# The down product of a layer on TensorE: eight of its ten tiles by seven products at two levels, over halves of the whole sequence, with streamed weights

## The chip, the cores and the metric

The kernel runs on one core of a Trainium2 chip. The core has TensorE (matmuls, out of SBUF into PSUM), VectorE, ScalarE and GpSimd for everything else, and SyncE (SP), whose queue issues most transfers between HBM and SBUF. The metric is the device time of one execution in microseconds (us).

## The reference

The input x has 8 sequences of 1024 rows of 512 numbers, all float32. With xn the normalised x, the layer computes

```python
xn = _layernorm(x, axis=-1)
s = _L0_attn_ref(xn, ...)           # gated linear attention with decay, 3 heads, then @ Wo * out_scale
gate, up = ghost(xn, gate_idx), ghost(xn, up_idx)   # w = lut[idx]; x @ w.T ; 512 -> 1376
h = silu(gate) * up
g = _silu(ghost(h, down_idx))       # 1376 -> 512: the down product
x = x + s * g
```

The weights of the three "ghost" products are looked up in a table of 16 numbers by integer indices. The down product multiplies h, 1024 x 1376 in each sequence, by a matrix of 1376 x 512.

## The kernel before, in words

The program has two phases. **Phase 1** runs the attention for the eight sequences (`project`, `chunks`): TensorE is kept in a written-out order, and between its steps `build_some` advances a generator, `ffn_weights`, which looks up the weights of the feed-forward part on VectorE (`look_up`: three bit masks, a shift, eight leaves, seven predicated copies), forms sums of their blocks on GpSimd, and stores them in HBM. `build_some` takes one step at each place; what is left of the generator after the last sequence runs at once. The results of the attention go to HBM too (`bl_d`), as do the normalised x and sums of its blocks (`xs_d`).

**Phase 2** runs the feed-forward part for one sequence after the other. The 1376 rows of h are ten tiles of 128 and a tail of 96. `quads` makes tiles 0 to 7 (in all but the first sequence 8 and 9 too), `single` the tail, each with fewer products than the plain way: a product of two matrices in 2 x 2 blocks takes seven block products instead of eight, in Winograd's form, where sums of blocks take the place of some operands. In `quads` this is done at two levels. One outer product of the seven is a `Node`: it has four PSUM banks, `t[0]` to `t[3]`, and its seven inner products go into them in the order 1, 5, 6, 2, 7, 3, 4. Instead of adding everything later, it starts a bank from another one: ScalarE copies t[0] to t[1] after product 1 (`first`), product 6 accumulates on that (`sixth`), ScalarE copies t[1] to t[2], and VectorE adds the copy `e` of product 5 to t[1] and t[3] (`sixth`, `seventh`). The first two products of the following node are placed inside the node.

Then comes the down product, `down_pair`, for the chunks c and c + 4 of 128 rows. The two chunks, two halves of five tiles of h, and two halves of 256 columns of the output are the 2 x 2 blocks. So there are four pairs, seven products each, five matmuls of 128 x 128 by 128 x 256 each (L976). The weights with their sums, `wd_sb`, stay in SBUF through phase 2. The sums of blocks of h are made by `sums` on VectorE (L956 to L959), for the first pair from inside `single`: `at_last` is called there, between the products 7 and 3 of the tail of h, and ahead of the two VectorE operations (L710, L713) that read the last products. The ScalarE Silu L711 reads what L710 writes, GpSimd's L714 multiplies. After the down products come a matmul with `wdt` (the tail), a Silu, a matmul `ps` of the attention's output by Wo (L998), a multiplication with it (L999), GpSimd's addition of x (L1001) and the store (L1002).

At the end `keep_order` ties every instruction of TensorE, VectorE, ScalarE and GpSimd to the one traced before it on the same engine. So these four run in the order of the program text; the order of the loads in SP's queue is left to the compiler's scheduler, except in the first part of phase 1.

PSUM has eight banks, two for each of the roles s11, s12, s21, sE. `ring` holds three buffers for streamed weights; `xs` (the x of the sequence with its sums) has one buffer, filled again once its readers are through.

Of the kernel before, what the change touches and what calls it, by code (L numbers as in the profile page):

```python
# [9 lines left out]
F32 = mybir.dt.float32  # L10
# [7 lines left out]
P = 128  # L18
# [19 lines left out]
def recurrent_block(ctx: ExitStack, tc, x, wq, wk, wv, wo, wg, decay_logits, out_scale, lut, gidx, uidx, didx, out):  # L38
# [18 lines left out]

    nc = tc.nc
# [25 lines left out]
    wd_d = [dram.tile([P, 7 * V // 2], F32, name=f"wdd{j}", tag=f"wdd{j}") for j in range(NK)]  # L84
# [28 lines left out]
    def defer(parts, issue):  # L113
        later.append([parts, issue])
# [111 lines left out]
    def ffn_weights(build, pool, pair_pool):  # L226
# [5 lines left out]

        upper = []

        def gate_up(o):
# [19 lines left out]
            defer(3, lambda: nc.sync.dma_start(out=wgu_d[o], in_=wide))  # L255
# [31 lines left out]
        def down(j):  # L287
            idx = build.tile([P, NB], I32, name="idx", tag="idx", bufs=2)
            for a in range(2):
                nc.sync.dma_start(out=idx[:, ts(a, V)], in_=didx[ts(j + a * NK, P), :])  # L290
            yield
            t = pool.tile([P, 2 * NB], F32, name="wgu", tag="wgu", bufs=2)
            yield from look_up(build, t[:, : 2 * V], idx, P, 2 * V)
            b11, b12, b21, b22, t1, t2, t4 = (t[:, ts(k, V // 2)] for k in range(7))
            nc.gpsimd.tensor_tensor(t1, b12, b11, ALU.subtract)
            nc.gpsimd.tensor_tensor(t2, b22, t1, ALU.subtract)
            yield
            nc.gpsimd.tensor_tensor(b12, b22, b12, ALU.subtract)
            nc.gpsimd.tensor_tensor(t4, b21, t2, ALU.subtract)
            defer(3, lambda: nc.sync.dma_start(out=wd_d[j], in_=t[:, : 7 * V // 2]))  # L300

        jobs = [gate_up(o) for o in range(NO)] + [down_tail()] + [down(j) for j in range(NK)]
# [333 lines left out]
    def phase_2():  # L636
        with (
# [6 lines left out]
            tc.tile_pool(name="wdp", bufs=1) as wdp,  # L644
        ):
            wd_sb = [wdp.tile([P, 7 * V // 2], F32, name=f"wd{j}", tag=f"wd{j}") for j in range(NK)]
# [5 lines left out]
            def load_x(b):  # L652

                xs = fx.tile([P, 7, 7, H], F32, name=f"xs{b}", tag="xs")
                nc.sync.dma_start(
                    out=xs[:, :, 0:4, :], in_=xs_d[b].rearrange("p (k r) (s t) -> p k (r s) t", r=2, s=2)
                )
                return xs

            def sums_of_x(xs, apart=False):  # L660

                b11, b12, b21, b22, t1, t2, t4 = (xs[:, :, k, :] for k in range(7))
                todo = [(t1, b12, b11), (t2, b22, t1), (t4, b21, t2)]
                if apart:
                    for k in (1, 6, 5, 7, 2, 3, 4):
                        n = X_OF[k]
                        todo.append((b12[:, n], b22[:, n], b12[:, n]))
                else:
                    todo.insert(2, (b12, b22, b12))
                for o, x1, x2 in todo:  # L670
                    nc.gpsimd.tensor_tensor(o, x1, x2, ALU.subtract)  # L671
                    yield
# [275 lines left out]
            def blocks(h, c):  # L948

                return [h[:, ts(k, NK), ts(cc, P)] for cc in (c, c + NC // 2) for k in range(2)]  # L950

            def sums(b, h, c):
                t = [ring.tile([P, 14, P], F32, name=f"s{b}_{c}_{k}", tag="wr")[:, : 2 * NK] for k in range(2)]
                s1, s2, s3, s4 = (t[k // 2][:, ts(k % 2, NK)] for k in range(4))
                a11, a12, a21, a22 = blocks(h, c)
                nc.vector.tensor_tensor(s1, a21, a22, ALU.add)  # L956
                nc.vector.tensor_tensor(s2, s1, a11, ALU.subtract)
                nc.vector.tensor_tensor(s3, a11, a21, ALU.subtract)
                nc.vector.tensor_tensor(s4, a12, s2, ALU.subtract)  # L959
                return s1, s2, s3, s4  # L960

            def down_pair(b, c, h, h_tail, bl, t, following):

                cc = c + NC // 2
                a11, a12, a21, a22 = blocks(h, c)
                lhs = {1: a11, 2: a12, 3: t[3], 4: a22, 5: t[0], 6: t[1], 7: t[2]}
                gx = tmp.tile([P, 4, V], F32, name=f"gx{b}_{c}", tag=("p1", "u2")[c % 2])
                g1, g2 = gx[:, 0], gx[:, 1]
                pw = tmp2.tile([P, 4, V], F32, name=f"pw{b}_{c}", tag=("u3", "e5")[c % 2])
                pe, u3 = pw[:, 0], pw[:, 1]  # L970
                for n, k in enumerate((c, cc)):
                    nc.sync.dma_start(out=gx[:, 2 + n], in_=x[b, ts(k, P), :])

                def product(ps, k, start, stop):
                    for n in range(NK):
                        nc.tensor.matmul(  # L976
                            ps,
                            lhsT=lhs[k][:, n, :],
                            rhs=wd_sb[n][:, ts(D_OF[k], H)],
                            start=start and n == 0,  # L980
                            stop=stop and n == NK - 1,
                            skip_group_check=True,
                        )

                def tail(ps, k, start):
                    m = OCH[-1][1]
                    nc.tensor.matmul(  # L987
                        ps,
                        lhsT=h_tail[:m, ts(k, P)],
                        rhs=wd_tail[:m, :],  # L990
                        start=start,
                        stop=False,
                        skip_group_check=True,
                    )

                def result(k, g, xr):
                    ps = bank("sE", f"ps{b}_{k}")
                    nc.tensor.matmul(ps, lhsT=bl[:, ts(k, P)], rhs=wo_sb, start=True, stop=True)  # L998
                    nc.vector.scalar_tensor_tensor(g, ps, osc, g, ALU.mult, ALU.mult)  # L999
                    end = (b, k) == (B - 1, NC - 1)  # L1000
                    (nc.vector if end else nc.gpsimd).tensor_tensor(g, g, xr, ALU.add)  # L1001
                    (nc.sync if end else nc.gpsimd).dma_start(out=out[b, ts(k, P), :], in_=g)  # L1002

                d1, d2, d3 = (bank(r, f"d{r}{b}_{c}") for r in ("s11", "s12", "s21"))
                product(d1[:, :H], 1, True, False)
                product(d1[:, H:], 5, False, False)
                nc.scalar.copy(pe, d1)
                product(d3[:, :H], 6, True, True)
                nc.vector.tensor_tensor(pe[:, :H], d3[:, :H], pe[:, :H], ALU.add)
                product(d1[:, :H], 2, False, False)  # L1010
                product(d3[:, H:], 7, False, True)
                nc.vector.tensor_tensor(u3[:, :H], d3[:, H:], pe[:, :H], ALU.add)
                nc.gpsimd.tensor_tensor(u3[:, H:], u3[:, :H], pe[:, H:], ALU.add)
                t = following() if following else None
                product(d1[:, H:], 3, False, False)
                tail(d1, c, False)
                nc.scalar.activation(g1[:, :H], d1[:, :H], AF.Silu)  # L1017
                nc.vector.tensor_tensor(g1[:, H:], d1[:, H:], pe[:, :H], ALU.add)
                nc.scalar.activation(g1[:, H:], g1[:, H:], AF.Silu)
                tail(d2, cc, True)  # L1020
                product(d2[:, :H], 4, False, True)
                nc.vector.tensor_tensor(g2, d2, u3, ALU.add)
                nc.scalar.activation(g2, g2, AF.Silu)
                result(c, g1, gx[:, 2])
                result(cc, g2, gx[:, 3])
                return t

            xs = load_x(0)
# [5 lines left out]
            for b in range(B):  # L1034
# [6 lines left out]
                def at_last():  # L1041
                    got.append(sums(b, h, 0))
# [8 lines left out]
                if b == 0:  # L1051
                    nc.sync.dma_start(out=wd_tail[: OCH[-1][1], :], in_=wdt_d)
                    for src, dst in zip(wd_d, wd_sb):
                        nc.sync.dma_start(out=dst, in_=src)
                quads(b, xs, h)
                single(b, NO - 1, xs, h, h_tail, at_last, tmp2)
                t = got[-1]
                more = iter(())
                for c in range(NC // 2):
                    nxt = (lambda: sums(b, h, c + 1)) if c + 1 < NC // 2 else None  # L1060
                    t = down_pair(b, c, h, h_tail, bl, t, nxt)
                    if b + 1 < B:
                        if c == 0:
                            xs = load_x(b + 1)
                            more = sums_of_x(xs)
                        else:
                            some(more, 2)
# [45 lines left out]
```

## Time and profile before

| | |
|---|---|
| time, median of 3 runs | 2159.64 us (2159.61 to 2161.4) |
| profiled execution | 2158.71 us, span 2156.9 us |
| granted TensorE clock | 1.000 |
| TensorE busy | 2147.4 us, 9486 matmul instructions |
| weight loads busy | 1647.1 us |
| VectorE, ScalarE, GpSimd busy | 1158.4, 863.9, 979.8 us |
| down products, L976 | 2240 instructions, 286.7 + 222.9 us |
| tails and results, L987 and L998 | 256 instructions, 60.2 + 60.2 us |
| matmuls of quads, L737 | 3724 instructions, 715.1 + 136.5 us |
| moved by DMA | 316.83 MB, 147 GB/s |

A row of the page reads: line, engine, operation, output <- inputs, shapes, count | busy us, mean ns of one | idle of the engine just before them, and what ended it. Matmuls are pipelined, so the mean of one (379 ns at 256 columns) is from its start to its end, while the distance from one start to the next is shorter. A float32 matmul of the program appears as two instructions. The timeline's lines give the start, the time from the first start to the last end, and the number of instructions merged. In the timeline phase 2 begins at about 605 us.

### The profile page before, as it was taken

What the parts mean: (1) busy time and instruction counts of PE and PEld (TensorE: products, weight loads), DVE (VectorE), ACT (ScalarE), POOL (GpSimd) and SP (SyncE); (2) the same over time, 40 slices, a digit from 0 to 9 for tenths busy, and PEclk for the clock granted to TensorE, in tenths of its full rate; (3) what the DMA queues carried; (4) which work ended last, traced back from release to release, by engine and by line L of the source; (5) the groups of instructions that cost most, each with busy time, mean ns of one, the idle gap of its engine ahead of it and who ended that gap; (6) DMA issues with size and microseconds to landing.
All of it is one profiled execution on the core that took longest, in us unless ns stands there. A gap on an engine that the chain in (4) does not pass through costs nothing.

```text
span 2156.9 us, 26203 instructions
## 1 busy us (share of the span) xinstructions
PE 2147.4 (100%) x9486; PEld 1647.1 (76%) x9486; DVE 1158.4 (54%) x1701; ACT 863.9 (40%) x1900; POOL 979.8 (45%) x902
## 2 busy tenths in 40 slices
PE   9999999999999999999999999999999999999998
PEld 5666666666668778778878887887788688778876
DVE  6888687678645435534543453354345435533543
ACT  3666666666334214413431441243144124413521
POOL 2554545444244553634455452455435353634442
PEclk9999999999999999999999999999999999999999
DMA  8776654545374434434442443345244334434411
GB/s 193 192 196 177 205 199 153 186 147 162 114 297 154 145 106 150 141 115 138 150 155 96 145 149 117 130 154 169 75 152 149 130 117 154 129 119 149 156 57 54
DMA packets 145943, 316.83 MB, mean 147 GB/s; under 512 B 50867, under 2 KB 76214, under 8 KB 144790
## 3 DMA queue, kind: packets, MB, share of 16 engines
q1 hardware_dynamic: 135974, 290.50, 41.7%
q0 software_dynamic: 7728, 23.86, 3.0%
q8 instruction: 75, 1.23, 0.2%
q10 hardware_dynamic: 2112, 0.79, 0.1%
q14 instruction: 54, 0.44, 0.1%
HBM read 233.98 MB, written 81.14 MB: 146 GB/s over the span
## 4 chain that ended last, share of the span: by engine, by line
PE 98%; POOL 1%; issue 0%; ACT 0%; DVE 0%; DMA 0%; POOLq 0%
PE s L737 32%; PE ds L976 22%; PE pq L410 10%; PE pv L373 8%; PE sE L737 5%; PE fs L687 4%; PE po L538 4%; PE ds L987 2%; PE ps L998 2%; PE psc L516 2%; PE pu L524 2%; PE fsE L687 2%; PE pt L366 1%; PE pk L507 1%; PE sE L780 1%; PE s L780 1%
## 5 line engine op out<-in xcount | busy, mean ns | idle before, releaser
L737 PE MATMUL s<-xs,wq 128*128 128x256 f32 x3192 | 715.1, 379 | 0.0
L737 PEld LDWEIGHTS s<-xs,wq 128*128 128x128 f32 x3192 | 605.6, 190 | 94.1 <-issue 7.0
L976 PE MATMUL ds<-wd,s 128*128 128x256 f32 x1280 | 286.7, 379 | 0.0
L976 PEld LDWEIGHTS ds<-wd,s 128*128 128x128 f32 x1280 | 243.2, 190 | 33.1
L410 PE MATMUL pq<-xnT,wqk_sb 128*128 128x512 f32 x512 | 230.3, 592 | 0.0
L976 PE MATMUL ds<-wd,h 128*128 128x256 f32 x960 | 222.9, 379 | 0.0
L976 PEld LDWEIGHTS ds<-wd,h 128*128 128x128 f32 x960 | 182.3, 190 | 52.5 <-issue 27.1
L831 POOL TENSOR_TENSOR u<-u,e 128x512 f32<-128x512 f32 x64 | 79.8, 1268 | 276.1 <-DVE u L827 276.1
L760 DVE TENSOR_TENSOR s<-s,e 128x512 f32<-128x512 f32 x133 | 93.0, 700 | 202.2 <-ACT s L759 202.2
L373 PE MATMUL pv<-wvg_sb,xnT 128*128 128x387 f32 x512 | 177.5, 488 | 0.0
L1001 POOL TENSOR_TENSOR gx<-gx 128x512 f32<-128x512 f32 x63 | 80.3, 1274 | 184.3 <-DVE gx L999 183.6
L410 PEld LDWEIGHTS pq<-xnT,wqk_sb 128*128 128x128 f32 x512 | 92.4, 190 | 92.1 <-issue 91.8
L764 DVE TENSOR_TENSOR sE<-s,e 128x512 f32<-128x512 f32 x133 | 93.0, 699 | 102.6 <-PE s L737 102.6
L737 PE MATMUL sE<-xs,wq 128*128 128x256 f32 x532 | 136.5, 379 | 0.0
L352 POOL TENSOR_SCALAR rstd<-rstd 128x1 f32<-128x1 f32 x56 | 26.8, 479 | 238.2 <-ACT junk L351 237.6
L373 PEld LDWEIGHTS pv<-wvg_sb,xnT 128*128 128x128 f32 x512 | 92.7, 190 | 54.3 <-issue 1.9
L755 ACT COPY e<-sE 128x512 f32<-128x512 f32 x133 | 77.8, 585 | 136.1 <-PE sE L737 136.1
L671 POOL TENSOR_TENSOR xs<-xs 128x1792 f32<-128x1792 f32 (+1 forms) x38 | 127.9, 3380 | 1.0
L1017 ACT ACTIVATE gx<-ds 128x256 f32<-128x256 f32 x32 | 12.3, 383 | 285.9 <-PE ds L987 285.9
L759 ACT COPY s<-s 128x512 f32<-128x512 f32 x133 | 75.8, 570 | 96.6 <-PE s L737 96.6
L748 ACT COPY s<-s 128x512 f32<-128x512 f32 x133 | 75.8, 570 | 95.8 <-PE s L737 92.1
L737 PEld LDWEIGHTS sE<-xs,wq 128*128 128x128 f32 x532 | 101.1, 190 | 13.7
(169 smaller groups left out, 3298.2 us busy)
## 6 DMA issues: line engine op xcount, KB each, us to landing
wq<-quadd SPq DMA_DIRECT2D x112, 896.0 KB, 4.4
xs<-xsd SPq DMA_DIRECT2D x8, 3584.0 KB, 11.9
wq<-quadd SPq DMA_DIRECT2D x42, 448.0 KB, 3.8
x<-in_x SPq DMA_DIRECT2D x64, 256.0 KB, 5.9
xsd<-ts SPq DMA_DIRECT2D x8, 2048.0 KB, 7.0
gx<-in_x SPq DMA_DIRECT2D x64, 256.0 KB, 2.7
out<-gx POOLq DMA_DIRECT2D x63, 256.0 KB, 2.3
ga<-gTd SPq DMA_DIRECT2D x16, 768.0 KB, 4.9
```

What stands on the lines that cost most here:

```text
L373: nc.tensor.matmul(pv, lhsT=xnT[:, v, ts(c, P)], rhs=wvg_sb[:, v, :], start=(v == 0), stop=(v == NV - 1))
L410: nc.tensor.matmul(pq, lhsT=wqk_sb[:, v, ts(j, D)], rhs=xnT[:, v, ts(hf, U)], start=(v == 0), stop=(v == NV - 1))
L538: nc.tensor.matmul(po, lhsT=lh, rhs=rh, start=(n == 0), stop=(n == len(prods) - 1))
L671: nc.gpsimd.tensor_tensor(o, x1, x2, ALU.subtract)
L687: nc.tensor.matmul(ps, lhsT=w[:, 2 * W_OF[k] + n, :m], rhs=xs[:, X_OF[k], 2 * n : 2 * n + 2, :], start=start and n == 0, stop=stop and n == 1,
L737: nc.tensor.matmul(self.t[n][:, ts(a, H)], lhsT=self.w[:, a, (0, 1, 6, 2, 3, 4, 5)[i - 1], :], rhs=self.xs[:, X_OF[self.ks[a]], D_OF[i], : ...
L755: nc.scalar.copy(self.e, self.t[3])
L760: nc.vector.tensor_tensor(self.t[1], self.t[1], self.e, ALU.add)
L764: nc.vector.tensor_tensor(self.t[3], self.t[2], self.e, ALU.add)
L831: nc.gpsimd.tensor_tensor(o[:, n], o[:, n], other[:, n], ALU.add)
L976: nc.tensor.matmul(ps, lhsT=lhs[k][:, n, :], rhs=wd_sb[n][:, ts(D_OF[k], H)], start=start and n == 0, stop=stop and n == NK - 1, skip_grou ...
L1001: (nc.vector if end else nc.gpsimd).tensor_tensor(g, g, xr, ALU.add)
```

## The change

Tiles 0 to 7 of h now take the seven products at two levels, as in `quads`. The outer blocks are halves of the sequence (512 rows), halves of the eight tiles (four each), halves of the output's columns (256). Each of the seven outer products is a `DownNode` with seven inner products over 256 rows, two tiles and 128 columns; in each inner product four matmuls of 128 x 128 by 128 x 128. The tiles 8 and 9 enter at the outer level only (`rest`), eight matmuls of the same size per node. A node's weights, 896 KB, are loaded into `ring` when it is set up. Its left operands that are sums come from VectorE: `sum_of` (outer, 128 x 2560 in three parts) and `four_of` (inner, four sums of 512 elements), issued one at a time between the steps of the node ahead; `s2` becomes the operand of node 3 on GpSimd. The sums needed first are made by `sums_ahead`, which is called where `sums` was. The results of the nodes are gathered in `cl` and `cu`; the tails and results of all eight chunks follow the nodes. The x of the following sequence is loaded in four parts and its sums are made in pieces.

In phase 1 the sums of the second level are added to the building of the down weights, and the stores of `wgu_d` for tiles 0 to 7, eight of them, are left out.

```diff
+    wd_d = dram.tile([P, 7, 2, 7 * P], F32, name="wdd", tag="wdd")
+    wdl_d = dram.tile([P, 7 * V // 2], F32, name="wdld", tag="wdld")
...
-            defer(3, lambda: nc.sync.dma_start(out=wgu_d[o], in_=wide))
+            if o >= 4 * NQ:
+                defer(3, lambda: nc.sync.dma_start(out=wgu_d[o], in_=wide))
...
-        def down(j):
+        def down(rows, e, ends):
...
+            nc.gpsimd.tensor_tensor(pair[:, :, 0], b12, b11, ALU.subtract)
+            yield
+            nc.gpsimd.tensor_tensor(b12, b22, b12, ALU.subtract)
+            defer(3, lambda: nc.sync.dma_start(out=to[:, :, 0:2, :], in_=up))
+            yield
+            nc.gpsimd.tensor_tensor(pair[:, :, 1], b22, pair[:, :, 0], ALU.subtract)
+            yield
+            nc.gpsimd.tensor_tensor(pair[:, :, 2], b21, pair[:, :, 1], ALU.subtract)
+            defer(4, lambda: nc.sync.dma_start(out=to[:, :, 4:7, :], in_=pair[:, :, 0:3]))
+            for _ in range(3):
+                yield
+
+        jobs = [gate_up(o) for o in range(NO)] + [down_tail()]
+        jobs += [down((j, j + 4), j % 2, j > 1) for j in (0, 2, 1, 3)] + [down((8, 9), None, True)]
...
+            class DownNode:
+                def __init__(self, b, k, block, z):
...
+                    self.w = ring.tile([P, 2, 7, P], F32, name=f"wd{name}", tag="wr")
+                    nc.sync.dma_start(out=self.w.rearrange("p e t m -> p e (t m)"), in_=wd_d[:, D_OF[k], :, :])
...
+                def product(self, n, i, start=False):
+                    for a in range(2):
+                        for e in range(2):
+                            nc.tensor.matmul(
+                                self.t[n][:, ts(a, P)],
+                                lhsT=self.lhs[i][:, e, ts(a, P)],
+                                rhs=self.w[:, e, D_OF[i], :],
...
+                def first(self):
+                    self.product(0, 1, True)
+                    nc.scalar.copy(self.t[1], self.t[0])
...
+                def sixth(self):
+                    self.product(1, 6)
+                    nc.scalar.copy(self.t[2], self.t[1])
+                    nc.vector.tensor_tensor(self.t[1], self.t[1], self.e, ALU.add)
...
+            def sums_ahead(b, h):
+                a11, a12, a21, a22 = blocks(h)
+                z, todo = four_of(f"z{b}_1", a11)
+                s1, parts_1 = sum_of(f"sx{b}_1", "sx", a21, a22, ALU.add)
+                s2, parts_2 = sum_of(f"sy{b}_2", "sy", s1, a11, ALU.subtract)
+                todo += [p + (ALU.add,) for p in parts_1[:2]] + [p + (ALU.subtract,) for p in parts_2[:2]]
+                for o, x1, x2, op in todo:
+                    nc.vector.tensor_tensor(o, x1, x2, op)
+                return z, s1, s2, [parts_1[2] + (ALU.add,), parts_2[2] + (ALU.subtract,)]
...
+                node = DownNode(b, 1, a11, z1)
+                node.first()
+                node.fifth()
+                node.fifth_copy()
+                for i, k in enumerate(order):
...
+                    node.sixth()
+                    some(1)
+                    node.product(0, 2)
+                    node.rest(0)
+                    empty(node.t, 0)
+                    some(1)
+                    if following:
+                        following.first()
...
+                    node.seventh()
+                    some(1)
+                    node.product(1, 3)
+                    node.rest(1)
...
+                    beside(k)
+                for k in (2, 3):
+                    tail(k, next_bank(f"pd{b}_{k}"))
+                for k in range(4):
+                    result(k)
+                for k in range(4, NC):
+                    tail(k, next_bank(f"pd{b}_{k}"))
+                for k in range(4, NC):
+                    result(k)
...
                 def at_last():
-                    got.append(sums(b, h, 0))
+                    got.append(sums_ahead(b, h))
```

## The prediction

> **What bounds the kernel now.** I read the page first: engine totals, then the chain that ended last, then the rows of the lines that change, and last the timeline around the two places where the changed work begins.
>
> ```profile
> PE 2147.4 (100%) x9486; PEld 1647.1 (76%) x9486; DVE 1158.4 (54%) x1701; ACT 863.9 (40%) x1900; POOL 979.8 (45%) x902
> PE 98%; POOL 1%; issue 0%; ACT 0%; DVE 0%; DMA 0%; POOLq 0%
> L976 PE MATMUL ds<-wd,s 128*128 128x256 f32 x1280 | 286.7, 379 | 0.0
> ```
>
> TensorE is busy in the whole span, holds 98% of the chain, and the down products (L976) never waited (idle 0.0). So every TensorE nanosecond removed is gained, and every new TensorE wait is lost. The chain in order of time gives the rate:
>
> ```profile
> 1051.66 5.18 PE s L737 x24
> 1057.70 5.18 PE s L737 x24
> ...
> 1114.59 12.95 PE ds L976 x60
> 1133.14 12.95 PE ds L976 x60
> ...
> 1170.23 12.95 PE ds L976 x60
> ```
>
> 60 of the down instructions take 12.95 us, so one of 256 columns costs 215.8 ns (a float32 matmul is two instructions in the records). A pair of chunks comes every 18.54 us: 70 x 215.8 ns = 15.11, plus 8 instructions of 512 columns for the tails and results (L987, L998), 3.43. No stall is left in it. Now the price of 128 columns, from the timeline of the attention part:
>
> ```profile
> 145.98 0.83 PE L524 MATMUL pu<-v,ks 128*128 128x128 f32 x6
> 146.65 0.83 PE L538 MATMUL po<-qb,R 128*128 128x128 f32 x6
> 147.32 0.83 PE L538 MATMUL po<-pr,v 128*128 128x128 f32 x6
> 147.99 0.49 PE L507 MATMUL pk<-ident,kT 128*128 128x128 f32 x3
> ```
>
> 18 instructions start within 2.01 us, each with new weights: 111.6 ns apiece. Six pk and pt instructions of the same width, transposes, start faster, at about 109.
>
> **What the Trainium skill says.** TensorE: Matmul & The Clock Gate, section Back-to-back issue gap, gives N/2.4 + 2.5 ns. With two passes per float32 instruction that is 215.8 for 256 columns, which the trace shows to the digit, and 109.2 for 128, where ordinary matmuls show 111.6. The trace decides: 111.6. The same page, LDWEIGHTS, says 128 columns / 1.2 = 107 ns for a weight load. The trace shows 190 ns from start to end of one, but bursts with a new one every 111.6, so loads overlap and are just about covered. Section Architectural detail says that ScalarE and VectorE queues are strict FIFO; the trace agrees (below, the Silu of L711 follows its add, and nothing passes it). Section Part 1: The HAM clock gate says that after an idle window of about 3.4 us, free-running, the clock halves until a busy window has passed. The kernel before has no such gap after its start, so no run here shows it yet.
>
> **The change, part by part.**
>
> 1. TensorE work of down. Removed per batch: 4 pairs x 7 products x 5 matmuls = 140, 280 instructions x 215.8 = 60.42 us. Added: per node 7 products x 4 matmuls of eight tiles, and 8 for the other two: 36, seven nodes 252, 504 instructions x 111.6 = 56.25 us. Tails and results stay 16 of 512 columns. Gain 4.18 us a batch, **33.4 us** in eight. At 109.3 ns it would be 5.3 and 42.6; at 119.9 it is nothing.
>
> 2. The start of down. This is where I expect the gain to go. Today, in `single` (batch 1):
>
> ```profile
> 918.50 1.88 PE L687 MATMUL fsE<-xs,wr 128*96 128x512 f32 x4
> 918.77 0.69 DVE L706 TENSOR_TENSOR t<-fs,t 96x512 f32<-96x512 f32 x1 [4.46 <-PE fs L687]
> 919.38 0.81 DVE L956 TENSOR_TENSOR s<-h 128x640 f32<-128x640 f32 x1
> 920.22 1.88 PE L687 MATMUL fs<-xs,wr 128*96 128x512 f32 x4
> 921.94 2.32 PE L976 MATMUL ds<-wd,h 128*128 128x256 f32 x10
> 922.44 0.68 DVE L710 TENSOR_TENSOR ht<-fsE,t 96x512 f32<-96x512 f32 x1
> 923.15 0.63 ACT L711 ACTIVATE ht<-ht 96x512 f32<-96x512 f32 x1 [5.57 <-DVE ht L710]
> 926.51 0.58 ACT L1007 COPY pw<-ds 128x512 f32<-128x512 f32 x1 [2.72 <-PE ds L976]
> ```
>
> `at_last` puts the sums ahead of L710 in VectorE's queue. Today they are 4 operations of 640 elements, 919.38 to 922.44, and they delay L710 and the Silu of L711 without harm: ScalarE's next work, L1007, waits for products that end at 926.5. The change puts eight there: four of 512 (0.60 each, 0.72 for the one that follows its own input; scaled from 640 in 0.73 and 0.85) and four of 1024 (1.135; the same rate, and L467 has 1.21 for one from start to end): 7.06 us. L710 then starts at 926.44, its Silu runs 927.15 to 927.75, and only behind it in ScalarE's queue comes the first copy of the new node (t[1] from t[0], 256 wide, 0.37 as L879): done at 928.1. The node's sixth product accumulates on that copy. TensorE gets there after products 1 and 5, 16 x 111.6 ns past 921.94, at 923.7. **Wait 4.4 us a batch, 35.2 us in all.** Queued behind it: all later TensorE work. The bounds: 3.9 with ScalarE's operations overlapping more, 6 if VectorE runs slower beside GpSimd (L957's median is 1.23 where its least is 0.82).
>
> 3. The clock after that gap. Idle is about 4.2 us. Against a free window of 3.4 us, about one gap in four holds a whole one; then 3.4 to 6.8 us run at half clock, 1.7 to 3.4 us lost. An estimate by the clock gate section: two batches of eight, **5 us**; bounds 0 and 27.
>
> 4. The rest of the nodes. One takes 72 x 111.6 = 8.03 us. VectorE has at most, in node 6, six adds of 256 from PSUM (0.42 each), four of 512 (2.5 together) and three sums (2.9): 7.9 us; node 7 with ten adds has 6.7. Both fit, the first barely, and each wait of TensorE lies 12 to 20 instructions (1.3 to 2.2 us) behind its producer. GpSimd rewrites s2 for node 3 once node 6 is through: two of 1024 and one of 512, by L671, L831 and L267 about 2.4 + 2.4 + 1.3 = 6.1 us, under node 2's 8. Cost 0; if it fails, 0.6 us a batch. `c22` and the sums of the next x have two nodes of cover.
>
> 5. Streaming. 896 KB per node; the same size takes 4.4 us in quads and comes every 6 us there. The ring of three gives about 10 us. But the next x (3584 KB in four parts), 2 MB of x rows and four nodes' weights fall into four nodes, 32 us: 9.4 MB, 290 GB/s, and the xs row moved 3584 KB in 11.9 us, 308 GB/s. Cost taken 0, up to 1.5 us a batch if SP issues a load behind those.
>
> 6. Building the weights, in phase 1. The builder gets 19 + 7 x 48 + 8 = 363 steps beside the attention. Two of the new down jobs have six more steps each. What is left over runs at once at the boundary, ahead of phase 2 on VectorE:
>
> ```profile
> 603.37 1.29 DVE L221 COPY_PREDICATED leaf<-bit,leaf 128x1024 f32<-128x1024 uint8 x1
> 604.56 1.52 DVE L204 TENSOR_SCALAR leaf<-idx,lut_x,lut_sb 128x1024 int32<-128x1024 int32 x2
> 606.12 2.64 DVE L221 COPY_PREDICATED leaf<-bit,leaf 128x1024 f32<-128x1024 uint8 x2
> 608.79 1.30 DVE L221 COPY_PREDICATED wgu<-bit,leaf 128x1024 f32<-128x1024 uint8 x1
> ```
>
> Today six operations remain, to 610.1, and L699 at 612.04 is on time. Twelve steps more leave 18: two bit masks and a shift (0.69 each, the medians of L197 and L200), eight leaves at 0.76 and seven copies at 1.31: 17.4 us, to 620.8. L699 and the copy of L700 after it end at 622.2; product 7 waits for them and would start at 615.2. **7.0 us once**, plus **2.5** for the clock, as this gap surely holds an idle window. Bounds 4 and 13. SP's wait for the last store delays the loads behind it to about 630, before quads need them. GpSimd's extra sums in phase 1 (eight, about 2.2 us) lie in its idle time; the eight dropped stores of wgud save DMA only.
>
> 7. The end. GpSimd needs 1.27 + 0.56 us per result (L1001, L1002) where TensorE now delivers one in 0.86, so the last output is later by about **0.7**.
>
> Sum: -33.4 + 35.2 + 5 + 7.0 + 2.5 + 0.7 = +17.0 us. The profiled execution took 2158.7 (span 2156.9), so 2175.7; the median shown is 0.9 above it. I forecast **2176**.
>
> **Rivals.**
> - A short wait at the start, the side of faster: without part 2, and with it part 3, the sum is -33.4 + 10.2 = -23, 2137. For it: TensorE's count alone. Against: the order of the queues. It decides below a wait of 2.9 us; by 2.3 it is outside the noise.
> - The clock halves in each batch: +22 on the forecast, 2198. For it: gaps of equal length every 190 us; against: 4.2 us is little over a window.
> - Weights arrive late: 1.5 us a batch, +12, 2188. For it: 290 against 308 GB/s; against: parts of these loads can be issued early, as gx is at 911 today.
> - TensorE bound by weight loads over long runs: at 120 ns the gain is gone (2209). Against: 18 starts at an even 111.6.
> - The change does not do what it says: then 4032 instructions of 128 columns would not be there. I give that nothing.
>
> **How the numbers follow.** About 0.2% (4.3 us) is what a measurement of this kernel can tell from no change. Forecast 0.57, of which 0.08 ends within that; short wait 0.17, of which 0.12 is faster and 0.05 the same; clock in each batch 0.12; late weights 0.10; weight loads 0.04. Slower 0.49 + 0.12 + 0.10 + 0.04 = 0.75, same 0.13, faster 0.12. The range: with 109.3 ns (-9), no halving in down (-5) and a shorter gap at the boundary (-3) it is 2159; I reach to 2153 for part of the short waits. Above, halving in each batch and 0.6 us of late weights give 2203.
>
> **What would show it.** Right: 4032 matmuls of 128x128 at 111 to 112 ns in the chain; a TensorE wait of 4 to 5 us for a ScalarE copy eight times; a gap near 615 behind VectorE's look-up. Wrong: no wait at the node's sixth product, or waits for DMA of the weights, or a spacing of 120. Under 2155 the short-wait rival was right.

## The result and the profile after

The changed kernel takes 2228.57 us (median of 4 runs, 2227.89 to 2228.75), the kernel before 2160.05 us beside it: a ratio of 1.0316 with a 95% interval of 1.0298 to 1.0333. It is 68.5 us slower. I had forecast 16. The span of the profiled execution grew from 2156.9 to 2226.8 us, and the mean granted clock fell to 0.983.

The totals by engine and the chain that ended last, on the page of the changed kernel:

```profile
PE 2143.3 (96%) x11278; PEld 1694.4 (76%) x11278; DVE 1435.8 (64%) x2109; ACT 923.9 (41%) x2068; POOL 1086.2 (49%) x994
PE 86%; DVE 7%; DMA 3%; POOL 1%; issue 1%; ACT 1%; SPq 0%; POOLq 0%; DVEq 0%
```

TensorE is busy for 4 us less than before, in a span that is 70 us longer, and its share of the chain fell from 98% to 86%. The chain now runs through VectorE and DMA. The waits of TensorE say where (engine, line, tile <- what ended the wait: us in total, times, longest):

```profile
PE s12d L1026 <- ACT s12d L1048: 33.8, 8, 4.2
PE s12d L1026 <- DVE s12d L1060: 12.8, 8, 1.6
PE fs L721 <- DMA wr<-wgud: 8.4, 1, 8.4
PE po L566 <- DVE pr L546: 6.7, 3, 4.6
PE sEd L1037 <- DVE sEd L1064: 5.6, 7, 0.8
```

The first row is the wait that I had forecast: eight times, 4.2 us. The third row stands at the boundary of the two phases, where my sum has a wait of another cause; the other three are in no term of it. Here is the first one in the timeline, at the start of down in batch 2:

```profile
1145.37 2.35 DVE L1074 TENSOR_TENSOR sx<-h 128x1024 f32<-128x1024 f32 x2
1147.64 2.35 DVE L1074 TENSOR_TENSOR sy<-sx,h 128x1024 f32<-128x1024 f32 x2
1149.91 0.68 DVE L744 TENSOR_TENSOR ht<-fsE,t 96x512 f32<-96x512 f32 x1
1150.62 0.63 ACT L745 ACTIVATE ht<-ht 96x512 f32<-96x512 f32 x1 [9.58 <-DVE ht L744]
1151.16 0.36 ACT L1048 COPY s12d<-s11d 128x256 f32<-128x256 f32 x1
1151.57 2.08 PE L1026 MATMUL s12d<-wdd,z 128*128 128x128 f32 x8 [4.23 <-ACT s12d L1048]
1153.44 1.91 PE L1026 MATMUL s11d<-wdd,h 128*128 128x128 f32 x8
```

Read it from the bottom up. Product 6 (1151.57) waited 4.23 us for the copy L1048. That copy had to follow the Silu L745, and the Silu the VectorE operation L744, which stood behind the four sums of 1024. The last two rows show the price of the gap: eight instructions start 1.87 us apart, where at full clock it is 0.89.

Set against the kernel before, the 69.9 us of span divide by place: phase 1 ends 10.0 us later (`zs` at 614.81, before 604.80), the boundary between the phases adds 10.5, the end adds 7.0 (from TensorE's last result to the end of the span 12.7 us, before 5.7), and the eight batches the other 42.4, as one batch period went from 192.49 to 198.0 us.

### The profile page after: what moved, and what is told of

Its sections match the earlier page's. It is cut to its first block, busy times and chain, and to the rows that moved or that the text cites. A ratio compares the mean times of both kernels' runs of the same rounds, so it can differ in the third digit from the quotient of the medians.

```text
span 2226.8 us, 30728 instructions
## 1 busy us (share of the span) xinstructions
PE 2143.3 (96%) x11278; PEld 1694.4 (76%) x11278; DVE 1435.8 (64%) x2109; ACT 923.9 (41%) x2068; POOL 1086.2 (49%) x994
## 4 chain that ended last, share of the span: by engine, by line
PE 86%; DVE 7%; DMA 3%; POOL 1%; issue 1%; ACT 1%; SPq 0%; POOLq 0%; DVEq 0%
PE s L771 31%; PE pq L438 8%; PE pv L401 6%; PE sE L771 5%; PE s12d L1026 4%; PE s21d L1026 4%; PE s11d L1026 4%; PE po L566 3%; PE fs L721 3%; PE pd L1133 2%; PE ps L1140 2%; DVE sx L1175 2%; PE psc L544 2%; PE sEd L1026 2%; PE pu L552 1%; PE sEd L1037 1%
## 5 line engine op out<-in xcount | busy, mean ns | idle before, releaser
L705 POOL TENSOR_TENSOR xs<-xs 128x512 f32<-128x512 f32 (+2 forms) x122 | 170.8, 1424 | 2.4
L1026 PE MATMUL s12d<-wdd,z 128*128 128x128 f32 x896 | 126.7, 287 | 46.6 <-ACT s12d L1048 33.8
L1026 PEld LDWEIGHTS s12d<-wdd,z 128*128 128x128 f32 x896 | 114.8, 201 | 49.7 <-ACT s12d L1048 35.4
L1169 POOL TENSOR_TENSOR sy<-h,sy 128x1024 f32<-128x1024 f32 (+1 forms) x24 | 61.3, 2570 | 138.4 <-PE s21d L1026 62.6
L869 POOL TENSOR_TENSOR h<-h,e 128x512 f32<-128x512 f32 x64 | 80.0, 1274 | 57.5 <-issue 46.4
L546 DVE TENSOR_TENSOR pr<-psc,w_tab 128x384 f32<-128x384 f32 x64 | 35.6, 556 | 109.2 <-PE psc L544 109.0
L721 PE MATMUL fs<-xs,wr 128*96 128x512 f32 (+1 forms) x200 | 92.4, 602 | 8.4 <-DMA wr<-wgud 8.4
```

What stands on the lines that cost most here:

```text
L721: nc.tensor.matmul(ps, lhsT=w[:, 2 * W_OF[k] + n, :m], rhs=xs[:, X_OF[k], 2 * n : 2 * n + 2, :], start=start and n == 0, stop=stop and n == 1,
L869: nc.gpsimd.tensor_tensor(of_h(half, n), of_h(half, n), two(other[:, n]), ALU.mult)
L1026: nc.tensor.matmul(self.t[n][:, ts(a, P)], lhsT=self.lhs[i][:, e, ts(a, P)], rhs=self.w[:, e, D_OF[i], :], start=start and a == 0 and e == ...
```

## The experiments

Each run was set against the kernel before on the same chip. The differences below are to the 2228.57 us of the changed kernel.

### The start of down

**e1_start: only the first inner sums stay ahead of the Silu.** The sums of 1024 elements are taken out from ahead of L744; `at_last` is called a second time for the two of s1 after the tail, and those of s2 go to the end of node 1's list.

```diff
+                if o == NO - 1:
+                    at_last(True)
...
-                todo += [p + (ALU.add,) for p in parts_1[:2]] + [p + (ALU.subtract,) for p in parts_2[:2]]
...
+                behind = [p + (ALU.add,) for p in parts_1[:2]]
+                rest = [parts_1[2] + (ALU.add,), parts_2[2] + (ALU.subtract,)]
+                return z, s1, s2, rest + [p + (ALU.subtract,) for p in parts_2[:2]], behind
```

> Edit: ahead of the last two VectorE operations of the tail of h only the four sums of node 1 (512 elements each) are left; the two sums s1 (1024) follow those operations, the two of s2 are spread into node 1. Theory (the first copy of node 1 on ScalarE sits behind the Silu of the tail, and that behind eight VectorE sums; the half clock follows from the gap): the eight waits of 4.4 us and the eight slow stretches of about 2.3 us both go, 54 us less, about 2175 us. Rival 1 (product 6 waits for its own operand z, not for the copy): the four sums are still ahead, so under 10 us go, 2219 or more. Rival 2 (the slow stretch has a cause of its own): only the waits go, about 2193 us.

Measured: 2185.83 us (ratio 1.0123, interval 1.0108 to 1.0138), 42.7 us less, clock 0.995. The wait for ScalarE is gone in all eight batches and so is the half clock behind it; the order of VectorE's queue was the cause. Of the 54 us that I expected, 11 are missing. A new wait took 10.7 us, 14 when it is counted from start to start with its slow restart; 3.9 us less in phase 1 (`zs` at 610.89), where nothing was edited, hide the rest. The new wait among TensorE's waits and in the timeline of this kernel (its node lines are 2 higher than the changed kernel's, `sum_of` operations 3):

```profile
PE s11d L1028 <- issue: 10.7, 7, 2.1
```

```profile
1139.83 6.30 POOL L705 TENSOR_TENSOR xs<-xs 128x512 f32<-128x512 f32 x4 [1.57 <-DMA xs<-xsd]
1141.57 1.76 DVE L1178 TENSOR_TENSOR z<-sx,z 128x512 f32<-128x512 f32 x1
1147.92 1.13 PE L1028 MATMUL s11d<-wdd,sy 128*128 128x128 f32 x8 [2.08 <-issue]
```

"issue" means that the profile shows no event that ended the wait; the operand of that product is `sy`, whose sums now stand in VectorE's queue behind sums that run beside GpSimd's L705. A VectorE sum of 512, 0.68 us alone, takes 1.76 there.

**e2_warm and e5_warm2: the clock apart from the wait.** Eighteen dummy products (36 instructions of 128 columns, whose sum is never read) fill TensorE's gap, so that the wait is kept and the idle time is not.

```diff
+                def keep_warm(self, n):
+                    for i in range(n):
+                        nc.tensor.matmul(
+                            self.spare[:, ts(i % 4, P)],
+                            lhsT=self.lhs[1][:, 0, :P],
+                            rhs=self.w[:, 0, 0, :],
...
+                node.keep_warm(18)
```

The first try, e2_warm, put them into the spare half of the bank t[0].

> Edit: 18 matmuls of 128x128 into an unused half of a PSUM bank (36 instructions, about 4.0 us) fill the gap between the products 5 and 6 of node 1; their sums are read by nothing. Theory (the clock halves because TensorE is idle for 4.2 us): the wait stays, now filled, the slow stretches go, 8 x 2.3 = 18 us less, about 2210 us, and the granted clock comes to 0.99 or more. Rival (the stretch is slow because its operands or weights are late): about 2228 us as after.

Measured: 2253.0 us (1.0434, 1.0419 to 1.045), 24.4 us more. The place was ill chosen: ScalarE's copy reads t[0], and the dummies themselves waited for that copy instead of running ahead of it.

```profile
1155.09 5.91 PE L1027 MATMUL s11d<-wdd,h 128*128 128x128 f32 x36 [4.23 <-ACT s12d L1061]
1160.84 1.06 PE L1039 MATMUL s12d<-wdd,z 128*128 128x128 f32 x8
```

It shows something all the same: 36 instructions at 111.6 ns with the last one's tail are about 4.2 us, they took 5.91, and the node's own product behind them is at full rate. The slow stretch belongs to the gap, not to the work that follows it.

e5_warm2 puts them into the bank of t[2], as in the diff above.

> Edit: as e2_warm, but the 18 matmuls that fill the gap write to the bank of t[2], which nothing reads or writes at that moment, so they can start at once (in e2_warm they wrote to the bank that ScalarE was copying, and waited with product 6). Theory (the clock halves because TensorE is idle): they fill the 4.4 us, products 6 and 2 of node 1 then run at 0.89 us per eight, 8 x 2.3 = 18 us less than after, about 2210 us. Rival (the stretch is slow from its own operands, or the clock does not count such matmuls): about 2228 us.

Measured: 2208.31 us (1.0227, 1.0212 to 1.0243), 20.3 us less, clock 0.996, and TensorE's wait for ScalarE is almost covered:

```profile
PE s12d L1039 <- ACT s12d L1061: 1.7, 8, 0.2
```

A period fell from 198.0 to 195.79 us although the work behind the copy begins no earlier. So the half clock alone costs 2.2 us a batch, 18 in all. The remaining 2 to 3 us of the gain lie in phase 1, which ended at 611.80.

### The nodes

**e3_nogp: GpSimd doesn't rewrite s2.** The computation leaves out the three GpSimd operations that turn s2 into the operand of node 3; node 3 uses s2 as it is.

```diff
-                            nc.gpsimd.tensor_tensor(o, x1, o, ALU.subtract)
+                            pass
```

> Leaves out: GpSimd's rewriting of s2 into the left operand of node 3 (three operations per sequence), so node 3 multiplies another operand. Theory (in nodes 2 and 7 the sums on VectorE take twice as long while GpSimd works on SBUF, and the add behind them is late): the waits of 1.6 and 0.8 us in front of the products 3 and the rest of node 2 go, with what is lost around them 2.7 us a sequence, up to 21 us less, about 2208 us; less of it if the sums of the next x on GpSimd move into that place. Rival (VectorE is simply full in node 6, 7.9 of 8.0 us, whatever GpSimd does): the waits stay, 2225 or more.

Measured: 2201.76 us (1.0197, 1.0182 to 1.0212), 26.8 us less, and both of TensorE's waits for VectorE in the nodes (12.8 and 5.6 us) are gone. The timelines show why. First the changed kernel, where the last two of the three sums for node 7's operand (`sx`) run beside GpSimd's L1169:

```profile
1177.81 2.83 POOL L1169 TENSOR_TENSOR sy<-h,sy 128x1024 f32<-128x1024 f32 x1 [7.83 <-PE s21d L1026]
1178.68 3.04 DVE L1175 TENSOR_TENSOR sx<-h 128x1024 f32<-128x1024 f32 x1
1180.59 2.25 POOL L1169 TENSOR_TENSOR sy<-h,sy 128x512 f32<-128x512 f32 x1
1181.64 1.75 DVE L1175 TENSOR_TENSOR sx<-h 128x512 f32<-128x512 f32 x1
1182.80 1.71 POOL L705 TENSOR_TENSOR xs<-xs 128x512 f32<-128x512 f32 x1
1183.31 0.42 DVE L1060 TENSOR_TENSOR s12d<-s12d,ed 128x256 f32<-128x256 f32 x1
1183.64 1.42 DVE L1175 TENSOR_TENSOR z<-sx 128x512 f32<-128x512 f32 x1
1183.78 1.16 PE L1026 MATMUL s12d<-wdd,z 128*128 128x128 f32 x8 [1.59 <-DVE s12d L1060]
```

Then e3_nogp, two of the same operations with GpSimd quiet:

```profile
1170.24 1.22 DVE L1175 TENSOR_TENSOR sx<-h 128x1024 f32<-128x1024 f32 x1
1172.31 0.68 DVE L1175 TENSOR_TENSOR z<-sx 128x512 f32<-128x512 f32 x1
```

A sum of 1024 takes 1.22 us alone and 3.04 beside GpSimd; one of 512 takes 0.68 alone, 1.75 beside L1169 and 1.42 beside L705, GpSimd's next work. The addition L1060, one of whose inputs is in PSUM, keeps its 0.42 beside GpSimd, but stands behind the slow sums in VectorE's queue, and TensorE's product waits for it.

The ends of the rows show how the two engines share. L1169 ends at 1180.64, the VectorE sum that began under it 1.08 us later; the second L1169 ends 1.12 us after that sum, and the sum of 512 then 0.55 us after it. Each one gets on only when the other engine's instruction is over.

**e6_room: the sums moved, nothing left out.** Node 7's outer sum is made one node earlier, in node 5, whose results ScalarE copies, so that VectorE has less to do. GpSimd's sums of the next x, four behind each node from 6 on, now all come behind L1169: four after node 2 and twelve after `c22`.

```diff
-                    if k == 6:
-                        of[7], parts = sum_of(f"sx{b}_7", "sx", a11, a21, ALU.subtract)
+                    if k == 5:
+                        of[7], parts = sum_of(f"sx{b}_7", "e5", a11, a21, ALU.subtract)
...
-                    if n > 1:
-                        some(more, 4)
+                    some(more, {3: 4, 4: 12}.get(n, 0))
```

> Edit: the three sums of node 7's outer operand are made in node 5 instead of node 6 (into the room of e5, so the second x rows are loaded in node 3), and GpSimd's sums of the next x wait: four in node 2, twelve behind c22 after node 7. Nothing is left out. Theory (sums on VectorE double beside GpSimd's work): VectorE has no sum of 1024 beside GpSimd's rewriting any more, the waits of nodes 6 and 2 go, 8 x 2.7 = 21 to 27 us less, about 2204 us. Rival (the sums double anyway, wherever they stand, since GpSimd's work only moves): half or less of it, 2216 or more. A second one: the late sums of x delay the results on GpSimd and the next sequence waits, up to 2228.

Measured: 2200.75 us (1.0192, 1.0176 to 1.0207), 27.8 us less. The waits for VectorE are gone and the period is 194.46 us, 3.5 less than 198.0. The contention isn't gone. Node 7's first sum now meets the first of GpSimd's three operations (L1173 in this kernel), and sums of 512 still take 1.42 us:

```profile
1159.42 2.67 POOL L1173 TENSOR_TENSOR sy<-h,sy 128x1024 f32<-128x1024 f32 x1 [14.15 <-DVE z L1179]
1159.79 3.38 DVE L1179 TENSOR_TENSOR sx<-h 128x1024 f32<-128x1024 f32 x1
1173.06 1.42 DVE L1179 TENSOR_TENSOR z<-z,sx 128x512 f32<-128x512 f32 x1
```

What changed is how much slow work stands ahead of each addition that TensorE needs. So a rival of the expectation, that the sums double wherever they stand, was true in part, and yet no wait was left.

### Phase 1, the boundary and the end

**e4_steps: more builder steps in phase 1**, so that fewer VectorE look-ups are left at the boundary.

```diff
-                    build_some((b, k) > (0, 0) and 1 + (0 < b < B))
+                    build_some((b, k) > (0, 0) and (1 + (0 < b < B) if b < B else 3))
```

> Edit: three steps of the weight builder per chunk instead of one in the last eight chunks of the attention, so four are left over instead of twenty. Theory (at the boundary TensorE waits for the first weights of phase 2, whose load stands in SP's queue behind the stores of the late sums): the wait of 8.4 us and the 1.9 us of half clock after it go, about 2218 us. If the look-ups on VectorE then delay the last chunks, some of it comes back: up to 2225. Rival (the loads are late for the release of SBUF alone): the wait stays within 2 us, about 2228.

Measured: 2225.12 us (1.0308, 1.029 to 1.0325), 3.4 us less. The boundary wait is gone: `fs` starts 3.54 us after `zs`. But `zs` itself is at 622.14, 7.3 us later, as the added look-ups stand in VectorE's queue ahead of `pr`, which TensorE needs:

```profile
PE po L566 <- DVE pr L546: 12.8, 5, 4.6
```

**e10_direct: the two stores of the upper tile taken apart.** b11 is stored at once, and b22 - b12 gets a place in `pair`; the look-up's buffer `wgu`, of which there are two, no longer has to wait for GpSimd and a store behind it.

```diff
+            nc.sync.dma_start(out=to[:, :, 0, :], in_=b11)
...
-            nc.gpsimd.tensor_tensor(b12, b22, b12, ALU.subtract)
-            defer(3, lambda: nc.sync.dma_start(out=to[:, :, 0:2, :], in_=up))
+            nc.gpsimd.tensor_tensor(pair[:, :, 3], b22, b12, ALU.subtract)
+            defer(4, lambda: nc.sync.dma_start(out=to[:, :, 1, :], in_=pair[:, :, 3]))
```

> The changed kernel with the stores of the upper tile taken apart: b11 is stored at once and the difference b22 - b12 gets a place of its own in pair, so that the look-up's buffer is free earlier; the builder gets no more steps. This separates the two edits of the run that had both. Theory (the 8 us wait for the buffer near 522 us, and the slow clock behind it, make 7 to 8 of the 10.0 us that phase 1 lost; the wait for the first weights of phase 2 is the queue's order and stays): zs near 607 us, the wait for wr still 6 to 9 us, about 8 us less than the changed kernel, 2219 to 2222 us. Rival (the boundary's wait came from the same late store): both go, 2211.

Measured: 2221.44 us (1.0279, 1.0257 to 1.0301), 7.1 us less. What it removed is this place in the timeline of the changed kernel:

```profile
510.19 0.52 SPq L320 DMA_DIRECT2D wdd<-wgu  x1
...
521.98 0.81 DVE L207 TENSOR_SCALAR wgu<-idx,lut_x,lut_sb 128x1024 int32<-128x1024 int32 x1 [8.03 <-DMA wdd<-wgu]
...
526.94 1.65 PE L566 MATMUL po<-pr,v 128*128 128x128 f32 x6 [4.56 <-DVE pr L546]
```

The store L320 takes 11.66 us to land. VectorE's look-up waits 8.03 us for the buffer, the attention's `pr` is behind it in the queue, and TensorE stands for 4.56 us and then runs six instructions in 1.65 us where 0.83 is usual. In e10_direct the long wait and the slow stretch are gone (two waits for `pr` remain, of at most 1.6 us), but the boundary wait is still there:

```profile
608.04 3.70 PE L1226 MATMUL zs<-wo_sb,ident 128*128 128x512 f32 x8 [0.36 <-ACT bl L568]
619.01 5.84 PE L722 MATMUL fs<-xs,wr 128*128 128x512 f32 x8 [7.27 <-DMA wr<-wgud]
```

**e7_phase1: that edit and 14 more builder steps** at the place beside `project`, where no `pr` is near.

```diff
-                    build_some(busy * 2)
+                    build_some(busy * (2 + (b > 0 and k % 4 == 3)))
```

> Two edits in phase 1, at different times in it. The new b12 is written to the free fourth part of pair instead of over the upper tile, whose b11 is stored at once; and the builder gets 14 more steps in the sequences 1 to 7, so 6 are left at the boundary instead of 20. Theory (the look-up of the following job waits for the store of the upper tile, and that look-up holds up the attention; the first loads of phase 2 stand behind the stores of the last job): the wait of 4.6 us near 522 us with its half clock, about 7, and the 8.4 us plus 1.9 at the boundary go, 17 us less, about 2212 us. Rival (in e4_steps the time came back as later look-ups in the attention): at most 7 us, 2221 or more.

Measured: 2210.79 us (1.0239, 1.0222 to 1.0256), 17.8 us less: 7.1 by e10's edit, 10.7 by the steps. `zs` is at 606.89 and `fs` at 610.42 with no wait. The boundary in the changed kernel:

```profile
604.94 0.52 SPq L325 DMA_DIRECT2D wdd<-pair  x1
607.86 0.58 SPq L686 DMA_DIRECT2D xs<-xsd  x1
614.79 0.33 SPq L581 DMA_DIRECT2D bld<-bl  x1
...
615.16 0.90 SPq L712 DMA_DIRECT2D wr<-wgud  x2
...
626.96 5.47 PE L721 MATMUL fs<-xs,wr 128*128 128x512 f32 x8 [8.44 <-DMA wr<-wgud]
```

The first weights of phase 2 (`wr`) leave SP's queue at 615.16; in the kernel before the first was issued at 590.03. Ahead of it stand the store L325, which waited 8.2 us for GpSimd's last sum, `xs`, and the store of the attention's last result, which can only go when that is done. With 14 steps done earlier, L325 is out of the way: in e7_phase1 the first `wr` is issued at 592.12. VectorE's left-over look-ups ended at 630.6 and were covered by this wait.

**e8_end: the last sequence's additions shared.** VectorE makes every second one and SP stores it.

```diff
-                    end = (b, k) == (B - 1, NC - 1)
+                    end = b == B - 1 and k % 2 == 1
```

> The changed kernel with one edit at its end: in the last sequence VectorE makes every second addition of x and SP issues its store, as the changed kernel already does for the last result alone. Theory (GpSimd's 1.27 + 0.3 + 0.56 us per result and its pause make the end about 6 us later than before): about 6 us less than the changed kernel, 2222 to 2223 us, the last store issued 1 to 2 us after TensorE's last result instead of 8. Rival (the late end comes from the stores themselves or from TensorE's results): no change, 2228.

Measured: 2223.06 us (1.0289, 1.0267 to 1.0311), 5.5 us less. In the changed kernel GpSimd spends 2.15 us on each of the results it adds, with one pause of 2.88:

```profile
2211.89 0.57 POOL L1145 DMA_DIRECT2D out<-gx  x1 [2.88 <-issue]
...
2221.10 1.27 POOL L1144 TENSOR_TENSOR gx<-gx,cu 128x512 f32<-128x512 f32 x1
2222.67 0.56 POOL L1145 DMA_DIRECT2D out<-gx  x1 [0.30 <-POOL gx L1144]
```

TensorE was done at 2214.07, 12.7 us before the span's end; in e8_end these are 7.6 us, in the kernel before 5.7. The pause stays in e8_end (2.89 us), and what it waits for isn't shown.

### All repairs together

**e9_all: e1_start, e6_room, e7_phase1 and e8_end in one kernel.**

> Edit: e1_start, e6_room and e7_phase1 together, and in the last sequence every second addition of x on VectorE with its store from SP. Theory (four separate losses, each at its place, and beneath them a gain of 33 us that is there): -54 - 24 - 17 - 6 against after, about 2128 us, 0.985 of before. If the losses overlap or each one uncovers another wait of the same size: 2150 to 2170, no better than before.

Measured: 2129.35 us (2129.12 to 2130.13), a ratio of 0.9863 with an interval of 0.9848 to 0.9877: 1.4% faster than the kernel before. Its totals, chain, and all of TensorE's waits over 0.3 us:

```profile
PE 2115.7 (99%) x11278; PEld 1674.2 (79%) x11278; DVE 1425.4 (67%) x2112; ACT 923.5 (43%) x2068; POOL 1082.5 (51%) x988
PE 97%; POOL 1%; ACT 1%; issue 0%; DVE 0%; POOLq 0%; DVEq 0%; ACTq 0%
```

```profile
PE po L567 <- POOL qb L524: 2.3, 2, 1.5
PE warm L343 <- POOL nhalf L131: 1.4, 1, 1.4
PE po L567 <- DVE pr L547: 0.6, 1, 0.6
PE zs L1233 <- ACT bl L568: 0.4, 1, 0.4
```

The period is 188.34 us, 4.15 less than the 192.49 of the kernel before. e1's new wait on `sy` is gone too: e6's edit puts the GpSimd sums of L705, which ran beside VectorE's sums there, behind L1169.

The changed kernel and e9_all run the same 11278 matmul instructions in the same order, so their starts can be set side by side. Between the first start and the last, the changed kernel is 93.7 us slower: 35.1 in the eight waits for the copy, 22.5 in the 15 waits for VectorE in the nodes with the slow restart behind each, 17.7 in slow stretches of the batches, 10.4 at the boundary and 8.0 in phase 1. Nothing else is left.

## Why the prediction was wrong

The direction and the main wait were right; the range, up to 2203, was too low by 26 us. By the parts of the sum, in us:

| part | predicted | measured |
|---|---|---|
| 1 TensorE work | -33.4 | -33 (4.15 a batch in e9_all) |
| 2 start of down | 35.2 | 35.1 |
| 3 clock after it | 5 | 18 |
| 4 rest of the nodes | 0 | 22.5 |
| 6 boundary | 9.5 | 10.5, by another cause |
| 6 GpSimd in phase 1 | 0 | 10.0, of it 6.8 gone in e10_direct |
| 7 end | 0.7 | 7.0 |

Parts 2 to 4 are counted from start to start against e9_all. The list of waits has less (33.8 for part 2, 18.4 for part 4), as it counts from the end of the last matmul, and the next one would have started 0.17 us before that end. e6_room agrees: it has none of part 4's 22.5 us, and 3 us less of slow stretches (a mean clock of 0.81 instead of 0.78 in the 10 us behind its gaps). Part 5, the streaming, was right at 0: no load of `wdd` ended a wait of TensorE.

**Part 3** failed in its count. I took two gaps of eight to hold an idle window and had all eight as a rival with a chance of 0.12. The mean clock in the 10 us behind each gap of 4.23 us, from the windows of the trace, is 0.83, 0.76 and six times 0.77: 0.17 to 0.24 of these 10 us lost each time. In seven other kernels that kept the gap (all but e1_start, e5_warm2 and e9_all) it is 0.73 to 0.83 behind every one of 56 more. So the way I read the Trainium skill's page TensorE: Matmul & The Clock Gate, section Part 1: The HAM clock gate, an idle window that must lie whole inside the gap, does not hold here: a gap of 4.2 us halved the clock 64 times of 64. The trace shows the halving begin inside the gap of batch 2, about 2.07 us after TensorE stopped (in a row: the stretch and its length, TensorE's busy time and instructions, the granted clock, DMA):

```profile
1147.34:1149.40 2.06, 0.00 (x1) 1.00 0.95 354
1149.42:1151.50 2.08, 0.00 (x0) 0.50 1.05 434
```

In the traces of all twelve kernels, after the first 25 us, the clock was halved only at instants a multiple of 3.41 us apart. Of the stretches of 3.41 us between such instants that ran at full clock, each of the 81 in which TensorE was idle for 1.99 us or more was followed by half clock, and none of the 7387 with 1.96 us or less. A gap of 4.2 us that falls on two such stretches leaves at least 2.1 us in one of them, and one that falls on three covers the middle one whole. That is why it happened every time. e1's gaps in the batches, of 2.1 us at most, left 1.64 us or less in any stretch, and the clock stayed full; the eight matmuls behind the longest took 1.13 us, as against 1.06.

**Part 4** failed by a step that I had bounded with 0.6 us a batch: "VectorE has at most, in node 6, ... 7.9 us", against 8.03 of the node. The three sums that I had put at 2.9 us took 6.0 (1.22, 3.04 and 1.75). I had seen in part 2 that VectorE may run slower beside GpSimd (L957's 1.23 and 0.82) and used it there as a bound; here I put GpSimd's 6.1 us "under node 2's 8" without asking what it does to VectorE. A margin of 0.1 us was no cover. The Trainium skill has it: SBUF — State Buffer, section Who interferes with whom, says that a VectorE instruction with two SBUF inputs contends with a GpSimd instruction that reads SBUF, that one with at most one SBUF input doesn't, and that the port pair which the two share is an exclusive lock. The runs agree on which operations suffer (0.68 to 1.42 us, and 0.42 unchanged), and on the lock. In the changed kernel each of the 86 VectorE sums of 512 (from `sum_of` and `four_of`) that began while a GpSimd operation was under way ended 0.55 to 0.66 us after that operation, however long it had still to run, and each of the 8 sums of 1024 ended 1.08 us after it. In the other direction, each of the 70 GpSimd sums of 512 that began under a VectorE sum of 512 ended 1.12 to 1.14 us after it. A VectorE sum that had begun first kept the time that it takes alone (16 of 16). In all kernels 981 of 997 such sums ended in this way; in the other 16, of e1_start and e9_all, GpSimd's operation had itself begun under a VectorE sum, and the next sum, close behind that one, still went first. So, but for these, the second to come waits out the whole instruction of the first: the price of a short VectorE sum is set by the GpSimd instruction that it meets.

**Part 6** had the boundary's size by chance. I let TensorE wait for L699 (L733 in the changed kernel) behind VectorE's left-over look-ups. These were indeed left over, to 630.6, but TensorE was already waiting for `wr`, whose issue I had not followed through SP's queue: I wrote that SP's wait for the last store delays "the loads behind it ... before quads need them", and overlooked that the first weights of `single` are among those loads. That GpSimd's extra sums in phase 1 "lie in its idle time" was the other failed step: the time was idle on GpSimd, but the store behind them holds one of two buffers of the look-up, and VectorE's queue carries that wait to the attention.

**Part 7** had the right two durations, 1.27 and 0.56, and the rate at which TensorE delivers, but I charged one result with the difference. The eight results come in two groups of four, 6.88 us apart, and GpSimd takes seven of them. One costs it 2.15 us, with 0.3 between the addition and the store that I had left out, so it is behind by the end of the first group, and then comes the pause of 2.88.

Of the rivals, "the clock halves in each batch" was true, beside the forecast rather than instead of it. The short wait, late weights for the nodes and the weight-load bound were not seen: with 111.6 ns for 4032 instructions a batch gains 4.18 us, and e9_all gained 4.15.

What stays open: what the 2.88 us pause of GpSimd waits for; whether the order in SP's queue alone made `wr` late, which is read from the times of issue and not from a run that changes only that order; and the up to 5 us by which profiled executions differ in phase 1 with no edit there (`zs` at 610.7 to 616.0 in the changed kernel, e1, e2, e3, e5, e6 and e8), so that differences of a few us between single edits are no more certain than that.

## What to carry to other kernels

A cost of nothing needs its cover measured under the neighbour it will have: VectorE's durations of SBUF sums are to be taken from rows that run beside GpSimd if the change puts GpSimd there. The sums needn't be kept apart from GpSimd; it was enough to move them to where nothing that TensorE needs stood close behind (e6_room). When an operation is added to a queue in order, follow every engine behind it one step further, and the buffers that its store holds, to TensorE; and follow the first load of the next stage through SP's queue. Then repair before judging: the same 33 us of TensorE work saved were worth +3.2% or -1.4%, by where sums, stores and steps were put.

## What the runs showed of the hardware

- A VectorE sum with both inputs in SBUF took 2.1 to 2.6 times as long beside a GpSimd operation (0.68 to 1.42 or 1.75 us at 512, 1.22 to 3.04 at 1024), one with an input in PSUM no longer (0.42). The sum that came second ended 0.55 to 0.66 us (512) or 1.08 us (1024) after the GpSimd instruction that it met, in 94 cases of 94.
- A TensorE gap of 4.2 us cost 1.7 to 2.7 us more by the halved clock, 64 times of 64. Dummy products in the gap removed that. The halving followed stretches of 3.41 us with 1.99 us or more of idle time, and none with 1.96 us or less.
- A store of 896 KB from `wgu` took 11.66 us to land, where the four stores of that form had a median of 6.2 and the loads of `wdd` of the same size one of 4.7.
